# Bringing attention sums back to rows of nodes through DRAM and VectorE instead of TensorE transposes

## The chip, the cores and the metric

The kernel runs on one core of a Trainium2 chip. Its engines are TensorE (PE in the profile, with its weight loads as PEld), VectorE (DVE), ScalarE (ACT), GpSimd (POOL) and SyncE (SP, which here only issues transfers). The metric is the device time of one execution in microseconds (us), the median of several runs; lower is better.

## The reference, cut to what matters

Two layers act on x, which is 16 batches of 1024 nodes with 256 channels, all float32. The first is a graph convolution with two batch norms; the second is an attention with 4 heads of 64 channels. Each ends in a residual and a layer norm.

```python
def _L1_gnn_ref(x, para, adj, kv_w):
    ...                                    # g: the graph product, relu
    q = transpose(g).reshape(B, N, 4, 64).transpose(0, 2, 1, 3)
    kv = (x @ kv_w).reshape(B, N, 2, 4, 64).transpose(2, 0, 3, 1, 4)
    k, v = kv[0], kv[1]
    attn = softmax(einsum('bhnd,bhmd->bhnm', q, k) * scale)
    out = einsum('bhnm,bhmd->bhnd', attn, v)
    return out.transpose(0, 2, 1, 3).reshape(B, N, C)

x = _layernorm(x + _L0_gnn_ref(x, adj, ...))    # layer 0
x = _layernorm(x + _L1_gnn_ref(x, para, adj, kv_w))   # layer 1
```

The change touches the end of layer 1: what happens between the product of exponentials and values, and the last layer norm.

## The kernel before

A batch is worked on in two halves of 512 queries (`hf`), a half in two pairs of heads (`pair`), and a pair in four steps. In a step PE computes scores for two blocks of 128 keys, ACT takes exponentials (`e`), DVE adds them into `acc` (the denominators), and PE multiplies them with the values. The result `o` has channels on the partitions and queries along the row. The layer norm needs it the other way round, with nodes on the partitions, so `finish_a` turns it with four PE transposes for every 256 queries, and DVE multiplies the turned tile (in PSUM) with the reciprocal denominators.

```python
def scores(g): ...      # PE: s <- kT, qT, 64x64 blocks
def exps(g): ...        # ACT: e <- exp(s), 6 buffers of e
def sums(g):            # DVE: acc += e, two adds of 128x1024 per step
    ...
        nc.vector.tensor_add(ACC[b, hf, pair], ACC[b, hf, pair], E[g, a])

def attend(g):          # PE: o <- v, e
    ...
    if cp == NT // 2 - 1:                       # after a pair's four steps
        t = otp.tile([P, FB], F32, tag=f"ot{pair}", bufs=2 - pair, ...)
        o = O.pop((b, hf, pair))
        nc.scalar.copy(t, o[0])
        nc.vector.tensor_add(t, o[1], t)
        OT[b, hf, pair] = t

def dens(b, hf): ...    # PE: pd <- acc (sums over partitions); ACT: dt <- pd
def recips(b, hf): ...  # PE: pr <- dt (transposes); DVE: RD <- 1 / pr

def finish_a(b, j):     # j: 256 queries
    hf, k = divmod(2 * j, KB)
    p = ps_t.tile([P, 2, C], F32, tag="t", name="pf")
    for a in range(2):
        for pair in range(NP):
            nc.tensor.transpose(p[:, a, ts(pair, P)], OT[b, hf, pair][:, ts(k + a, P)], ident)
    r = ...
    nc.vector.tensor_mul(r, p, RD)              # 128x512, p in PSUM
    (nc.gpsimd if b < B - 1 else nc.vector).tensor_add(r, r, x1s.pop((b, j)))

def finish_s(b, j): ... # DVE: mean and variance of r; POOL: rs, nm
def finish_b(b, j): ... # ACT: r <- normalised; SP: out <- r
```

The normalised input of a later batch already takes another way into rows. Layer 0 leaves it in DRAM as `yT` with channels outside and nodes inside; `load` fetches it in pieces of 32 numbers so that each 32x32 block lies on the right partitions, POOL scales it (`bn2_q`), and one DVE instruction turns every 32x32 block (`rows`):

```python
y_blk = [yT_all[b].rearrange("i (d e) (q n) -> q e (i d) n", e=Q, q=NQ) for b in range(B)]  # Q = 32

def fetch_rows(b, j):   # called by load
    for q in range(NQ):
        nc.sync.dma_start(yts[b, j][q * Q : (q + 1) * Q]..., y_blk[b][q][:, ts(j, 2 * C // Q), :])
    nc.sync.dma_start(xrs[b, j], x[b, ts(j, 2 * P), :]...)

def bn2_q(b, j): ...    # POOL: yt <- yt * s, yt <- yt + t, 128x512 each
def rows(b, j):
    nc.vector.transpose(x1s[b, j], yts[b, j])
    nc.vector.tensor_add(x1s[b, j], x1s[b, j], xrs[b, j])
```

The pieces of later batches (`load`, `bn2_q`, `rows`, the gates `wg`, keys, values and the graph product) and the ends of earlier halves are put between groups of four steps by a hand-made schedule. A half batch ends every 8 steps. After the second half of a batch comes the stretch with the gates of the next batch and the loads and rows of the one after it; after the first half come only graph products, transposes of x1 and the ends. Every engine keeps its order of instructions, and all transfers are issued in order by SP.

Of the kernel before, what the change touches and what calls it, by code (L numbers as in the profile page):

```python
# [9 lines left out]
F32 = mybir.dt.float32  # L10
# [6 lines left out]
P = 128  # L17
# [5 lines left out]
def gnn_norm_attention_kernel(  # L23
# [16 lines left out]
    nc = tc.nc  # L40
    B, N, C = x.shape
    H = W1.shape[0]
    NT = N // P
    CT = C // P
    HT = H // P
    FB = 512
    NH = N // FB
# [4 lines left out]
    dram = ctx.enter_context(tc.tile_pool(name="dram", bufs=1, space=DRAM))  # L52
    ctx.enter_context(tc.manual_schedule())

    ident = const.tile([P, P], F32, name="ident")
# [25 lines left out]
    Q = 32  # L81
    NQ = P // Q
    y_blk = [yT_all[b].rearrange("i (d e) (q n) -> q e (i d) n", e=Q, q=NQ) for b in range(B)]
    st2_dram = dram.tile([2, C], F32, name="st2_d")

    c_dram = [dram.tile([NT, P], F32, name=f"crow_d{b}") for b in range(B)]
# [33 lines left out]
    with ExitStack() as l0:  # L120
# [32 lines left out]
        with ExitStack() as ph1:  # L153
# [9 lines left out]
            for i in range(0, NT, 2):  # L163
                t = hp.tile([P, 2, N], F32, tag="h", name=f"A{i}")
# [22 lines left out]
            KB = FB // P  # L187
# [6 lines left out]
            for h in range(NH):  # L194
                rows = range(h * KB, (h + 1) * KB)
                for i in rows:
                    blk = A[i][:, ts(i, P)]
# [8 lines left out]
                for j in range(NT):  # L206
                    p = ps.tile([P, FB], F32, tag="ah"[j % 2], name="pat")
# [25 lines left out]
            for c in range(HT):  # L233
                p = ps.tile([P, FB], F32, tag="a", name="pw1")
# [3 lines left out]
            for c in range(CT):  # L238
                p = ps.tile([P, FB], F32, tag="a", name="pw2")
# [120 lines left out]
            def hidden(b, h, f):  # L360
                p = ps.tile([P, FB], F32, tag="h", name="ph")
                for k in range(CT):
                    nc.tensor.matmul(
                        p,
                        W1T[:, k, ts(f, P)],
                        aggT[b][:, k, ts(h, FB)],
                        start=(k == 0),
                        stop=(k == CT - 1),
                    )
                return p  # L370
# [11 lines left out]
            for f in range(HT):  # L382
                for h in range(NH):
# [3 lines left out]
                    p = hidden(B - 1, h, f)  # L387
# [51 lines left out]
        with ExitStack() as ph2:  # L439
# [74 lines left out]
            for k, pair in enumerate(pairs):  # L514
# [4 lines left out]
                if not ahead:  # L519
                    for j in range(LDP):  # L520
                        load(0, j)
                    for j in range(LDP, NT // 2):
                        t = accp.tile([P, 2, FB], F32, tag="acc", name=f"first{j}")
# [14 lines left out]
    NP = HEADS // 2  # L538
# [17 lines left out]
    def fast():  # L556
      with ExitStack() as fx:
# [9 lines left out]
        otp = pool("otp", 3)  # L567
# [3 lines left out]
        ps_t = pool("ps_t", 4, space=PSUM)  # L571

        x1s, x1Ts, css, crows, mvs, wgs = {}, {}, {}, {}, {}, {}
        kTs, qTs, vs, S, E, ACC, O, OT, DT = {}, {}, {}, {}, {}, {}, {}, {}, {}
# [152 lines left out]
        def step(g):  # L727
            b, s = divmod(g, NS)
            hf, pair, cp = s // (NP * NT // 2), s // (NT // 2) % NP, s % (NT // 2)
            return b, hf, pair, cp  # L730
# [22 lines left out]
        def sums(g):  # L753
# [4 lines left out]
            else:  # L758
                for a in range(2):
                    nc.vector.tensor_add(ACC[b, hf, pair], ACC[b, hf, pair], E[g, a])  # L760

        def attend(g):
            b, hf, pair, cp = step(g)
            if cp == 0:
                O[b, hf, pair] = [ps_t.tile([P, FB], F32, tag="t", name=f"o{g}_{r}") for r in range(2)]
            for a in range(2):
                cb = 2 * cp + a
                for r in range(2):
                    for h in range(2):
                        nc.tensor.matmul(  # L770
                            O[b, hf, pair][r][h * HD : (h + 1) * HD, :],
                            vs[b][r * HD : (r + 1) * HD, cb, pair * P + h * HD : pair * P + (h + 1) * HD],
                            E[g, a][r * HD : (r + 1) * HD, h, :],
                            start=(cb == 0),
                            stop=(cb == NT - 1),
                        )
                E.pop((g, a))
            if cp == NT // 2 - 1:
                t = otp.tile([P, FB], F32, tag=f"ot{pair}", bufs=2 - pair, name=f"ot{g}")
                o = O.pop((b, hf, pair))  # L780
                nc.scalar.copy(t, o[0])  # L781
                nc.vector.tensor_add(t, o[1], t)  # L782
                OT[b, hf, pair] = t

        def dens(b, hf):
            p = ps_t.tile([P, FB], F32, tag="t", name="pd")
# [10 lines left out]
        KB = FB // P  # L797

        def recips(b, hf):
# [5 lines left out]
                RD[:, i : i + KB, :], p.rearrange("p k (h r) -> p k h r", r=32)[:, :, :, 0]  # L805
            )

        def finish_a(b, j):
            hf, k = divmod(2 * j, KB)
            p = ps_t.tile([P, 2, C], F32, tag="t", name="pf")  # L810
            for a in range(2):
                for pair in range(NP):
                    nc.tensor.transpose(p[:, a, ts(pair, P)], OT[b, hf, pair][:, ts(k + a, P)], ident)  # L813
            pool_r = (rp, "r") if b < B - 1 else (x1p, "x1")
            r = pool_r[0].tile([P, 2, C], F32, tag=pool_r[1], name=f"r_{b}_{j}")
            rd = RD[:, b * NT + 2 * j : b * NT + 2 * j + 2, :].rearrange("p a h -> p (a h)")
            nc.vector.tensor_mul(  # L817
                r.rearrange("p a (h d) -> p (a h) d", h=HEADS),
                p.rearrange("p a (h d) -> p (a h) d", h=HEADS),
                rd.unsqueeze(2).to_broadcast([P, 2 * HEADS, HD]),  # L820
            )
            (nc.gpsimd if b < B - 1 else nc.vector).tensor_add(r, r, x1s.pop((b, j)))  # L822
            R[b, j] = r
# [52 lines left out]
        def put(w, t, f, *a):  # L876
            at.setdefault(w * NC + t, []).append((f, a))
# [4 lines left out]
        for b in range(B):  # L882

            for hf in range(NH):
                t = (hf + 1) * (NC // NH)
                put(b, t, dens, b, hf)
                put(b, t + 1, recips, b, hf)
                for k in range(KB // 2):
                    put(b, t + 1 + k, finish_a, b, hf * (KB // 2) + k)
                    put(b, t + 1 + k, finish_s, b, hf * (KB // 2) + k)  # L890
                    late = NC - t - 2 - k if b == B - 1 and hf == 0 else 0
                    put(b, t + 2 + k + late, finish_b, b, hf * (KB // 2) + k)
            if b == 0:
                continue

            put(b - 2, 2, begin, b)
            for j in range(NT // 2):
                put(b - 2, j, load, b, j)
                put(b - 2, j + 1, bn2_q, b, j)
                put(b - 2, j + 2, rows, b, j)  # L900
                put(b - 2, j + 2, ln1_a, b, j)
                put(b - 2, j + 3, ln1_b, b, j)
                put(b - 2, j + 4, x1_t, b, j)
            put(b - 2, NC - 2, means, b)
            put(b - 2, NC - 1, crow, b)

            i = 0
            for t, n in enumerate(WG):
                for i in range(i, i + n):
                    put(b - 1, t, wg_a, b, i)  # L910
                    put(b - 1, t, wg_b, b, i)
                i += 1
            kv = [(keys, (b, c, h)) for c in range(CT) for h in range(NH)]
            kv += [(values, (b, j)) for j in range(0, NT, 2)]
            for t, n in enumerate(KV):
                for _ in range(n):
                    f, a = kv.pop(0)
                    put(b - 1, t, f, *a)
            m = 0
            for t, n in enumerate(QG):  # L920
                for m in range(m, m + n):
                    put(b - 1, NC - len(QG) + t, graph, b, m)
                m += 1
# [3 lines left out]
        nsteps = B * NS  # L927


        order = (dens, recips, finish_a, finish_b, x1_t, rows, ln1_a, ln1_b, finish_s, means, load, crow)  # L930
        rank = {f: k for k, f in enumerate(order)}
        short = (dens, recips, finish_a, x1_t, crow)
        long = (keys, values, graph)

# [120 lines left out]
        for t in range(min(at) // 2, max(max(at) // 2, nsteps // NK - 1) + 1):  # L1055
            g = NK * t
            now = [p for s in (2 * t, 2 * t + 1) for p in [(opening, (s,))] + arrange(at.get(s, []))]
            behind = max((k + 1 for k, fa in enumerate(now) if fa[0] in short), default=0)
            for k in range(len(now) + 1):
                if k == behind and 0 <= g < nsteps:  # L1060
                    sums(g)
                if k < len(now):
                    f, a = now[k]
                    f(*a)
            for k in range(g, g + NK):
                if 0 <= k + 1 < nsteps:
                    scores(k + 1)
                    exps(k + 1)
                if 0 <= k < nsteps:
                    if k > g:  # L1070
                        sums(k)
                    attend(k)
# [6 lines left out]
        )  # L1079

    flag = fast()


# [153 lines left out]
```

## Time and profile before

| | before |
|---|---|
| time, median of 3 runs | 2548.84 us (2546.09 to 2551.68) |
| span of the profiled execution | 2546.3 us |
| PE busy | 2487.9 us, 98% |
| DVE busy | 1730.6 us, 68% |
| ACT busy | 1078.3 us, 42% |
| POOL busy | 865.3 us, 34% |
| transfers | 233,349 packets, 163.79 MB, 21.1% of 16 engines' span on SP's queue |

Busy time is the union of an engine's instructions; share is of the span. The profile's groups list instructions of one source line together, with the tile written and the tiles read (`acc<-acc,e`), the mean duration of one and the idle time of the engine ahead of them with what ended it. The timeline lists the same instructions in order of time, with equal neighbours merged. Matmuls are pipelined, so what one costs PE is read from the distance of starts, not from its duration.

### The profile page before, as it was taken

How to read it: one execution, taken by the hardware profiler on the slowest of the kernel's cores; microseconds unless marked ns; L12 is line 12 of the kernel's file. 1: busy time of each engine (PE TensorE's matmuls, PEld its weight loads, DVE VectorE, ACT ScalarE, POOL GpSimd, SP SyncE). 2: the span in 40 equal slices, each digit the busy share in tenths (PEclk: the TensorE clock that was granted, in tenths of full speed). 3: DMA queues.
4: the chain of work that ended last, by engine and by line, in shares of the span. 5: the costliest groups of instructions: out<-in, count | busy, mean ns of one | idle time of the engine just before them, and what ended most of it. 6: DMA issues, size and time to landing. Idle time of an engine off the chain costs nothing. (4 is left out here: it accounts for less than half of the span.)

```text
span 2546.3 us, 33280 instructions
## 1 busy us (share of the span) xinstructions
PE 2487.9 (98%) x12813; PEld 1067.4 (42%) x12813; DVE 1730.6 (68%) x2594; ACT 1078.3 (42%) x1385; POOL 865.3 (34%) x766
## 2 busy tenths in 40 slices
PE   8999999998998999999999999999999999999997
PEld 4444444443443444344443444434444344443432
DVE  5545554556776776786877768777687776877556
ACT  2000000004453455465554655546556465564644
POOL 2222322222555323342433324333243332432132
PEclk9999999999999999999999999999999999999998
DMA  3122222230885201111111111111111111110000
GB/s 132 66 89 93 99 74 91 83 141 21 301 297 173 59 18 46 43 29 34 26 46 46 26 34 26 46 46 26 34 26 46 47 25 34 27 48 27 9 13 23
DMA packets 233349, 163.79 MB, mean 64 GB/s; under 512 B 136680, under 2 KB 221280, under 8 KB 226016
## 3 DMA queue, kind: packets, MB, share of 16 engines
q1 hardware_dynamic: 233184, 161.60, 21.1%
q8 instruction: 103, 1.69, 0.3%
q14 instruction: 62, 0.51, 0.1%
HBM read 98.58 MB, written 62.98 MB: 63 GB/s over the span
## 5 line engine op out<-in xcount | busy, mean ns | idle before, releaser
L751 ACT ACTIVATE e<-s 128x1024 f32<-128x1024 f32 x512 | 495.8, 1020 | 361.9 <-PE s L739 311.5
L760 DVE TENSOR_TENSOR acc<-acc,e 128x1024 f32<-128x1024 f32 x384 | 515.8, 1343 | 72.7 <-ACT e L751 42.6
L739 PE MATMUL s<-qT,kT 64*64 64x512 f32 x4096 | 492.4, 596 | 13.9 <-ACT e L751 13.2
L770 PE MATMUL o<-e,v 64*64 64x512 f32 x4096 | 486.4, 590 | 0.0
L713 PE MATMUL pg<-wg,x 128*128 128x512 f32 x960 | 434.5, 594 | 0.0
L822 POOL TENSOR_TENSOR r<-r,x 128x512 f32<-128x512 f32 x60 | 105.7, 1761 | 572.3 <-ACT wg L671 261.1
L739 PEld LDWEIGHTS s<-qT,kT 64*64 64x64 f32 x4096 | 147.2, 133 | 309.6 <-issue 250.9
L770 PEld LDWEIGHTS o<-e,v 64*64 64x64 f32 x4096 | 157.0, 133 | 284.1 <-issue 271.4
L599 POOL TENSOR_TENSOR yt<-yt,stq 128x512 f32<-128x512 f32 x120 | 192.4, 1603 | 193.2 <-DMA yt<-yT 188.3
L713 PEld LDWEIGHTS pg<-wg,x 128*128 128x128 f32 x960 | 172.3, 190 | 175.9 <-issue 166.1
L98 ACT COPY u<-pa 128x512 f32<-128x512 f32 x15 | 8.8, 585 | 475.3 <-PE pa L303 475.3
L680 DVE SCALAR_TENSOR_TENSOR wg<-wg,adj_sb 128x1024 f32<-128x1024 f32 x128 | 156.3, 1239 | 67.3 <-ACT wg L676 65.0
L303 PE MATMUL pa<-AhT,x 128*128 128x512 f32 x360 | 161.8, 592 | 0.0
L688 PE MATMUL pk<-x1T,kvw 128*128 128x512 f32 x256 | 118.4, 606 | 1.3 <-DVE x1T L639 1.3
L639 ACT COPY x1T<-px 128x512 f32<-128x512 f32 x60 | 35.1, 586 | 191.4 <-PE px L638 190.6
L699 PE MATMUL pv<-kvw,x1T 128*128 128x256 f32 x512 | 115.7, 379 | 0.0
L721 DVE TENSOR_TENSOR qT<-pg,para_sb 128x512 f32<-128x512 f32 x64 | 44.2, 690 | 101.7 <-PE pg L713 100.8
L334 PE MATMUL ph<-agg,SW 128*128 128x512 f32 x240 | 112.8, 592 | 0.0
L66 POOL TENSOR_SCALAR rs_a<-mv_a 128x2 f32<-128x2 f32 x64 | 20.5, 320 | 258.3 <-DVE mv_a L548 258.3
L303 PE MATMUL pa<-T,sx 128*128 128x512 f32 x240 | 107.9, 592 | 0.0
L303 PEld LDWEIGHTS pa<-AhT,x 128*128 128x128 f32 x360 | 68.4, 190 | 86.1 <-issue 86.1
L782 DVE TENSOR_TENSOR ot<-o,ot 128x512 f32<-128x512 f32 x64 | 44.0, 688 | 87.8 <-ACT ot L781 87.8
(193 smaller groups left out, 3332.4 us busy)
## 6 DMA issues: line engine op xcount, KB each, us to landing
h<-hT SPq DMA_DIRECT2D x28, 1024.0 KB, 4.4
hL<-h SPq DMA_DIRECT2D x28, 1024.0 KB, 9.2
x<-in_x_dram SPq DMA_DIRECT2D x16, 1024.0 KB, 7.3
yT<-y SPq DMA_DIRECT2D x64, 256.0 KB, 2.5
out_dram<-r SPq DMA_DIRECT2D x64, 256.0 KB, 2.1
xr<-in_x_dram SPq DMA_DIRECT2D x62, 256.0 KB, 2.9
yt<-yT SPq DMA_DIRECT2D x240, 64.0 KB, 2.9
crow<-crow_d SPq DMA_DIRECT2D x15, 512.0 KB, 4.0
```

Of the source, the lines that this page charges most:

```text
L303: nc.tensor.matmul(p, xs[n][:, k, :], bs[n][:, k, :], start=(k == 0), stop=(k == KN - 1))
L334: nc.tensor.matmul(p, ws[n][:, ts(f, P)], bs[n], start=True, stop=True)
L599: nc.gpsimd.tensor_tensor(y, y, sc, op)
L680: nc.vector.scalar_tensor_tensor(t, t, 1.0, adj_sb[:, i, :], op0=OP.add, op1=OP.mult)
L688: nc.tensor.matmul(p, kvw[:, k, ts(c, P)], x1Ts[b][:, k, ts(h, FB)], start=(k == 0), stop=(k == CT - 1))
L699: nc.tensor.matmul(p[:, ts(a, C)], x1Ts[b][:, k, ts(j + a, P)], kvw[:, k, C:], start=(k == 0), stop=(k == CT - 1),)
L713: nc.tensor.matmul(pg[b], x1s[b, k // 2][:, k % 2, ts(c, P)], wgs[b, k][:, ts(h, FB)], start=(k == 0), stop=(k == NT - 1))
L739: nc.tensor.matmul(t[r * HD : (r + 1) * HD, h, :], kTs[b, pair][h * HD : (h + 1) * HD, ts(2 * cb + r, HD)], qTs[b, pair, hf][h * HD : (h + ...
L751: nc.scalar.activation(E[g, a], S.pop((g, a)), AF.Exp)
L760: nc.vector.tensor_add(ACC[b, hf, pair], ACC[b, hf, pair], E[g, a])
L770: nc.tensor.matmul(O[b, hf, pair][r][h * HD : (h + 1) * HD, :], vs[b][r * HD : (r + 1) * HD, cb, pair * P + h * HD : pair * P + (h + 1) * HD],
L822: (nc.gpsimd if b < B - 1 else nc.vector).tensor_add(r, r, x1s.pop((b, j)))
```

## The change

Sums of values take the way that the input of a batch already takes. The finished tile `ot` goes from SBUF to a DRAM tile `o`, is read back in pieces of 32 numbers so that its 32x32 blocks lie on the right partitions, and one DVE instruction turns all blocks. This is meant to free PE from the four transposes of each `finish_a`. Only the second half of the last batch keeps the PE transposes, since nothing is left there to hide a way through DRAM. The second buffer of `ot0` is given up and its room taken by `ob`, the tile that is read back.

```diff
+    o_dram = {(b, h): dram.tile([NT // NH, C, P], F32, name=f"o{b}_{h}") for b in range(B) for h in range(NH)}
...
+        def by_pe(b, hf):
+            return b == B - 1 and hf == NH - 1
...
             if cp == NT // 2 - 1:
-                t = otp.tile([P, FB], F32, tag=f"ot{pair}", bufs=2 - pair, name=f"ot{g}")
+                t = otp.tile([P, FB], F32, tag=f"ot{pair}", bufs=1, name=f"ot{g}")
...
-                OT[b, hf, pair] = t
+                if by_pe(b, hf):
+                    OT[b, hf, pair] = t
+                else:
+                    nc.sync.dma_start(
+                        o_dram[b, hf][:, ts(pair, P), :].rearrange("i p n -> p i n"),
+                        t.rearrange("p (i n) -> p i n", n=P),
+                    )
...
+        def fetch_o(b, j):
+            hf, k = divmod(2 * j, KB)
+            if by_pe(b, hf):
+                return
+            t = OB[b, j] = otp.tile([P, 2, C], F32, tag="ob", bufs=1, name=f"ob{b}_{j}")
+            blk = o_dram[b, hf].rearrange("i (d e) (q n) -> q e (i d) n", e=Q, q=NQ)
+            for q in range(NQ):
+                nc.sync.dma_start(
+                    t[q * Q : (q + 1) * Q].rearrange("p a (d n) -> p (a d) n", n=Q),
+                    blk[q][:, ts(k // 2, 2 * C // Q), :],
+                )
...
         def finish_a(b, j):
...
+            if by_pe(b, hf):
+                p = ps_t.tile([P, 2, C], F32, tag="t", name="pf")
+                ...                                     # the four PE transposes
+            else:
+                p = r
+                nc.vector.transpose(r..., OB.pop((b, j))...)
             nc.vector.tensor_mul(r, p, RD)              # p is now r itself, in SBUF
...
                 for k in range(KB // 2):
+                    put(b, t + k, fetch_o, b, hf * (KB // 2) + k)
                     put(b, t + 1 + k, finish_a, b, hf * (KB // 2) + k)
...
-        order = (dens, recips, finish_a, finish_b, x1_t, rows, ln1_a, ln1_b, finish_s, means, load, crow)
+        order = (dens, recips, finish_a, fetch_o, finish_b, x1_t, rows, ln1_a, ln1_b, finish_s, means, load, crow)
```

More of the change, by code (lines that the diff above doesn't have):

```diff
@@ L806, in recips @@
             )
+        OB = {}
+        def fetch_o(b, j):
[9 more added lines that the diff above has]
+                )
         def finish_a(b, j):
             hf, k = divmod(2 * j, KB)
[L810 to L813, printed above, removed]
             pool_r = (rp, "r") if b < B - 1 else (x1p, "x1")
             r = pool_r[0].tile([P, 2, C], F32, tag=pool_r[1], name=f"r_{b}_{j}")
+            if by_pe(b, hf):
+                p = ps_t.tile([P, 2, C], F32, tag="t", name="pf")
+                for a in range(2):
+                    for pair in range(NP):
+                        nc.tensor.transpose(p[:, a, ts(pair, P)], OT[b, hf, pair][:, ts(k + a, P)], ident)
+            else:
+                p = r
+                nc.vector.transpose(
+                    r.rearrange("p a c -> p (a c)"), OB.pop((b, j)).rearrange("p a c -> p (a c)")
+                )
             rd = RD[:, b * NT + 2 * j : b * NT + 2 * j + 2, :].rearrange("p a h -> p (a h)")
```

## The prediction

> **What bounds the kernel now.** I read the page's shares first, then PE's waits, then the groups by shape, and last the timelines of PE and DVE over one batch in the middle (1618 to 1723 us; one batch takes 1723.34 - 1617.54 = 105.8 us from its second-half denominators to the next). The page:
>
> ```profile
> PE 2487.9 (98%) x12813; PEld 1067.4 (42%) x12813; DVE 1730.6 (68%) x2594; ACT 1078.3 (42%) x1385; POOL 865.3 (34%) x766
> ...
> PE   8999999998998999999999999999999999999997
> ...
> DVE  5545554556776776786877768777687776877556
> ```
>
> PE is busy in nearly every slice, DVE at about 0.7 in the attention slices. PE's longest listed wait is small:
>
> ```profile
> PE s L739 <- ACT e L751: 13.2, 16, 4.8
> ```
>
> That is 13.2 us in the whole run, so at first sight PE alone sets the time, and whatever is taken from PE is won. The groups by shape give the durations for the sums below (columns: busy us, mean ns of one, idle us ahead):
>
> ```profile
> L760 DVE TENSOR_TENSOR acc<-acc,e 128x1024 f32<-128x1024 f32 x384 | 515.8, 1343 | 72.7 <-ACT e L751 42.6
> ...
> L604 DVE TENSOR_TENSOR x<-x,xr 128x512 f32<-128x512 f32 x60 | 53.5, 891 | 2.1
> ...
> L817 DVE TENSOR_TENSOR r<-pf,RD 128x512 f32<-128x512 f32 x64 | 43.8, 684 | 39.3 <-PE pf L813 39.2
> ...
> L603 DVE STREAM_TRANSPOSE x<-yt 128x512 f32<-128x512 f32 x60 | 42.1, 702 | 0.0
> ...
> L813 PE MATMUL pf<-ident,ot 128*128 128x128 f32 x256 | 40.2, 280 | 0.0
> ```
>
> But the timeline of PE shows a second limit. It holds the stretch after a second half (from 1618):
>
> ```profile
> 1642.77 0.66 PE L813 MATMUL pf<-ident,ot 128*128 128x128 f32 x4
> 1643.26 5.35 PE L699 MATMUL pv<-kvw,x1T 128*128 128x256 f32 x24
> ...
> 1665.87 1.90 PE L770 MATMUL o<-e,v 64*64 64x512 f32 x16
> 1667.70 2.12 PE L791 MATMUL pd<-acc,ones 128*32 128x512 f32 x8
> 1669.75 0.66 PE L638 MATMUL px<-ident,x 128*128 128x128 f32 x4
> ```
>
> The denominators' matmul pd takes 2.12 us here and 1.07 us elsewhere (at 1617.54 and 1723.34). It is waiting for the last acc. DVE in the same stretch:
>
> ```profile
> 1627.18 1.22 DVE L680 SCALAR_TENSOR_TENSOR wg<-wg,adj_sb 128x1024 f32<-128x1024 f32 x1 [1.12 <-ACT wg L676]
> 1628.32 0.68 DVE L817 TENSOR_TENSOR r<-pf,RD 128x512 f32<-128x512 f32 x1
> ...
> 1631.31 0.43 DVE L547 BATCH_NORM_STATS2 st_z<-r 128x6 f32<-128x256 f32 x1 [1.17 <-POOL r L822]
> ...
> 1645.10 0.68 DVE L817 TENSOR_TENSOR r<-pf,RD 128x512 f32<-128x512 f32 x1
> ...
> 1659.53 9.18 DVE L760 TENSOR_TENSOR acc<-acc,e 128x1024 f32<-128x1024 f32 x6
> 1668.63 0.68 DVE L782 TENSOR_TENSOR ot<-o,ot 128x512 f32<-128x512 f32 x1
> ...
> 1676.03 0.26 DVE L804 RECIPROCAL RD<-pr 128x16 f32<-128x16 f32 x1 [2.32 <-PE pr L802]
> 1679.05 0.69 DVE L817 TENSOR_TENSOR r<-pf,RD 128x512 f32<-128x512 f32 x1 [2.76 <-PE pf L813]
> ```
>
> From 1631.31 to 1673 DVE has no gap at all, and its acc ends at 1668.71, after PE has arrived at 1667.70. So between 1631 and 1669 **DVE is the bound**, by a hair, and PE by a hair less. After the first half (1669 to 1723) DVE waits 2.32 and 2.76 us for PE: there PE is the bound. The 2.12 us form of pd stands in the timeline once per batch, 13 times in all, in the batches whose stretch holds the loads and rows of a batch two ahead.
>
> [...] L604, with both inputs in SBUF, goes from 691 up to 1269 ns, mean 891, while L817, whose pf is in PSUM, stays at 679 to 692. [...] Pieces of 32 numbers are 128 B; the trace has the same pattern already (the two groups below), at a small price.
>
> **The change, part by part.**
>
> Taken from PE: 64 - 2 = 62 groups of four transposes. By distance of starts one group costs 1626.38 - 1625.94 = 0.44 us (first of a half) or 1643.26 - 1642.77 = 0.49 us (second). 31 x 0.44 + 31 x 0.49 = 28.8 us.
>
> Added to DVE: 62 block transposes. L603 is the same instruction, 0.70 us: 43 us of busy time. The multiplication now reads r from SBUF instead of pf from PSUM: alone 0.69 as before, beside POOL like L604, so up to +0.2 us. DVE busy 1731 to about 1780.
>
> Added transfers: per half two stores of 256 KB and eight fetches of 64 KB. The existing pairs are:
>
> ```profile
> yT<-y SPq DMA_DIRECT2D x64, 256.0 KB, 2.5
> ...
> yt<-yT SPq DMA_DIRECT2D x240, 64.0 KB, 2.9
> ```
>
> SP needs about 0.5 us to issue each fetch (four in 2.1 us). So after ot (end 1618.95): store landed about 1621.3, four fetches issued by 1623.4 and landed by about 1626, since in the trace POOL starts on a fetched tile 4.05 us after the first of its four issues (1655.61, 1659.66). DVE wants the tile at 1628.3. After a first half it is 1669.3 + 7.1 = 1676.4 against a slot of 1676.3 to 1679. **The way through DRAM is hidden**, with up to about 2 us to spare.
>
> Moved: SP issues in order, and the loads of the batch two ahead stand behind the store and the first fetch. Before they were issued at 1603; now from 1623.4, landing about 1627.4. POOL's two bn2_q (1.6 to 2.0 us each) then run until about 1631.2 ahead of POOL's add of r (2.1 us), which before ended at 1631.28 and now at about 1633.4. DVE's schedule also changes: one gate (0.66 + 1.2 us) now stands ahead of the st_z that waits for it, and fills that wait. DVE: transpose 1628.3, multiplication (contended) to 1630.0, acc 1631.2, gate 1633.1, st_z 1633.4 to 1634.5, second gate, accs from 1635.7. Before: 1635.37. So the first block transpose of this stretch costs only about 0.3 us, because it falls where DVE waited anyway.
>
> The second transpose (at 1645) has no such gap: +0.74 us. POOL's later work overlaps more of the six accs, which are slowed by it (9.2 us contended, 7.9 us for six in the other half): +0.3 to 0.4. DVE's chain in this stretch thus grows by D = 0.3 + 0.75 + 0.35 = about 1.4 us, and PE, who had two groups of transposes less there (0.93 us), waits for it.
>
> Sum: of the 62 groups 26 (2 x 13) lie in those stretches and give nothing; the other 36 give 28.8 - 13 x 0.93 = 16.7 us. Against that stand 13 x 1.4 = 18.2 us of longer DVE chain. Net **+1.5 us: 2550 us**.
>
> **Rivals.**
>
> *PE is the bound everywhere.* Then all 28.8 us are won: 2520 us. For it: 98% busy, waits of 13 us. Against it: the long pd and the gapless DVE stretch. If D were 0, 2532 us.
>
> *The transfer is late, and DVE, in order, stands before it with everything behind.* Each microsecond costs 13 in the stretches after second halves; after first halves DVE has gaps. Fetches and loads now queue together (eight fetches in 4 us), and a row copy in front (crow) slowed such a set to 5.2 us in the trace. Two us late: 2576 us.
>
> *POOL becomes the gate.* If the loads land at 1629 instead of 1627.4, r, st_z and the accs come 1.6 us later, and 13 x 1.6 = 21 us are lost: 2571 us. I take this as the likeliest way to be wrong upwards.
>
> **Range and chances.** D decides. At D = 0 it is 2532, at 1.4 it is 2550, at 3.5 it is 2578. With some room below for waits on PE that go away too: 2528 to 2580. Two per cent is 51 us; faster than 2498 needs more than PE can give (28.8 us), so 0.03; slower than 2600 needs D above 5, so 0.05; within 0.92.
>
> **What would show it.** PE's busy time down by about 29 us and its idle time up by about as much; waits of PE for DVE (acc at pd, or wg at the graph product pg) appearing once per batch in the stretch after a second half; that stretch (1617.5 to 1669.8, 52.2 us) longer by about 1.4 us and the rest of the batch (53.6 us) shorter by about 0.9; DVE's transposes of ob at about 702 ns with little wait for the DMA; DVE's multiplication near 0.75 to 0.9 us. If DVE waits for ob, or PE's idle time stays as it was, the steps above are wrong.

## The result and the profile after

The change makes the kernel slower: **2580.48 us** (median of 4 runs, 2578.87 to 2581.23) against 2547.47 us beside it (2546.06 to 2551.68). The ratio is 1.0126 [1.0108, 1.0144]. That is within 2%, as predicted, but 30 us above the predicted 2550, at the upper edge of the range (2580). The profiled spans are 2546.3 and 2577.0 us.

The page after the change, busy time by engine and VectorE's row of tenths:

```profile
PE 2469.6 (96%) x12565; PEld 1045.0 (41%) x12565; DVE 1790.3 (69%) x2656; ACT 1078.1 (42%) x1385; POOL 872.0 (34%) x766
...
DVE  5555555457676778686876868768687686876656
```

PE has 248 matmuls less (62 groups of four transposes) and is 18 us less busy, but the span is 31 us longer, so its idle time has grown by 49 us. The waits of PE say for whom (us in all, times, longest):

```profile
PE pg L714 <- DVE wg L681: 35.6, 13, 3.3
PE s L740 <- ACT e L752: 24.1, 16, 9.4
...
PE pd L803 <- DVE acc L761: 3.4, 3, 3.0
```

The first entry is new: the graph product waits for VectorE's gates 13 times, once in each batch that loads another one. The waits for ScalarE's exponentials were there before, 13.2 us in all and 4.8 at most; now one of them is 9.4 us long. Where do these waits stand? The distances of the denominators' matmul pd cut each trace into stretches (starts; "stretch" is from a second half's pd to the first half's, "rest" from there to the next second half's):

| | before | after, 5 of 13 batches | after, 8 of 13 |
|---|---|---|---|
| stretch with the loads | 50.16 | 52.59 | 54.26 |
| rest of the batch | 55.64 | 54.81 | 53.76 |
| batch | 105.80 | 107.40 | 108.02 |

The three columns are the usual batch of each kind (two pauses of about 3.3 and 2.9 us in the first group of five add some tenths). Over the 13 batches the sum is 1375.8 us before and 1402.4 after, +26.6. Outside them, up to the first of these batches the kernel gains 1.3 + 0.8 = 2.1 us, and after the last it loses 194.14 - 187.96 = 6.2 us. These add up to the 30.7 us of the spans. The 1.3 us stand ahead of the first pd (926.71 against 927.99 us), where two kernels that are alike up to there can differ as much (928.25 us with the added matmuls below), so they need not come from the change.

The next fence is PE's timeline in one batch of the last column (start, duration, operation; in brackets the wait ahead and what ended it):

```profile
1519.95 1.06 PE L803 MATMUL pd<-acc,ones 128*32 128x512 f32 x8
...
1557.59 1.13 PE L714 MATMUL pg<-wg,x 128*128 128x512 f32 x2 [2.67 <-DVE wg L681]
1558.65 3.32 PE L740 MATMUL s<-qT,kT 64*64 64x512 f32 x16
...
1574.24 1.06 PE L803 MATMUL pd<-acc,ones 128*32 128x512 f32 x8
```

After the pause a group of 16 score matmuls takes 3.32 us; elsewhere it takes 1.90 to 1.95. Its clock, by windows (stretch and length; busy us of PE, PEld, DVE, ACT, POOL; granted clock; DMA share; GB/s):

```profile
1555.00:1557.50 2.50, 0.00 (x0) 0.00 (x0) 2.43 (x6) 0.00 (x0) 2.37 (x3) 1.00 0.53 132
1557.50:1560.00 2.50, 2.41 (x10) 0.77 (x14) 2.46 (x4) 1.16 (x3) 2.40 (x4) 0.82 0.03 7
1560.00:1562.50 2.50, 2.50 (x16) 0.80 (x12) 2.40 (x10) 2.36 (x3) 1.95 (x4) 0.50 0.51 135
```

PE was idle in the first window and was then granted half its clock, by these windows for about (1 - 0.82) x 2.5 / 0.5 + 2.5 = 3.4 us. This is what tells the two columns apart: in 8 of the 13 batches the pause is followed by half speed, in 5 it is not, even where the pause was the longest (3.30 us). Note that the time at half speed counts as busy, so that PE's busy time fell by only 18 us.

VectorE in the same stretch (same columns as PE's timeline):

```profile
1530.73 0.70 DVE L845 STREAM_TRANSPOSE r<-ob 128x512 f32<-128x512 f32 x1
1531.47 0.80 DVE L849 TENSOR_TENSOR r<-r,RD 128x512 f32<-128x512 f32 x1
1532.19 2.07 DVE L758 TENSOR_TENSOR acc<-e,e 128x1024 f32<-128x1024 f32 x1
1534.18 1.76 DVE L674 TENSOR_SCALAR wg<-wg 128x1024 int32<-128x1024 int32 x1
...
1539.31 9.35 DVE L761 TENSOR_TENSOR acc<-acc,e 128x1024 f32<-128x1024 f32 x6
1549.18 0.70 DVE L845 STREAM_TRANSPOSE r<-ob 128x512 f32<-128x512 f32 x1
...
1564.37 9.18 DVE L761 TENSOR_TENSOR acc<-acc,e 128x1024 f32<-128x1024 f32 x6
```

The block transposes start at their slot, 0.70 us each and without a wait for the DMA; in none of the 13 stretches does one wait. The way through DRAM is hidden here. But the chain that begins at pd ends 1564.37 + 9.18 - 1519.95 = 53.60 us later. Before it ended 1659.53 + 9.18 - 1617.54 = 51.17 us later. **VectorE's chain has grown by 2.43 us, not by the predicted 1.4.** The first acc took 2.07 us and the gate's first instruction 1.76 us. Before, in the stretch from 1617.54, they took 1.22 and 0.66 us, and the six accs behind them began 17.83 us after pd in place of 19.36:

```profile
1628.92 1.22 DVE L757 TENSOR_TENSOR acc<-e,e 128x1024 f32<-128x1024 f32 x1
...
1632.40 0.66 DVE L673 TENSOR_SCALAR wg<-wg 128x1024 int32<-128x1024 int32 x1
...
1635.37 9.21 DVE L760 TENSOR_TENSOR acc<-acc,e 128x1024 f32<-128x1024 f32 x6
```

What GpSimd did in the changed kernel meanwhile:

```profile
1529.69 3.49 POOL L600 TENSOR_TENSOR yt<-yt,stq 128x512 f32<-128x512 f32 x2 [28.37 <-DMA yt<-yT]
1533.14 2.25 POOL L854 TENSOR_TENSOR r<-r,x 128x512 f32<-128x512 f32 x1
```

It scaled the loaded rows until 1533.18, beside most of the long acc, and then added x to r until 1535.39, beside most of the slow gate. In the batches without half speed pd usually starts 52.59 us after the last pd, 1.01 us before VectorE's chain ends (53.60), and has its long form (2.12 us): its second half needs the last acc. In the others PE comes about 0.6 us after the chain (54.26), and pd has its short form.

The two transfers, in the list of DMA issues (KB each, median us from issue to landing):

```profile
o<-ot SPq DMA_DIRECT2D x62, 256.0 KB, 2.3
...
ob<-o SPq DMA_DIRECT2D x248, 64.0 KB, 2.1
```

In the 13 batches the longest wait of a block transpose for its transfer is 2.00 us; it stands after a first half, and the rest of that batch is no longer for it (53.75 us). Only at the end of the run do the transfers show. VectorE's two longest waits for one, and two waits of PE:

```profile
2491.98 0.71 DVE L845 STREAM_TRANSPOSE r<-ob 128x512 f32<-128x512 f32 x1 [4.81 <-DMA ob<-o]
...
2533.79 0.71 DVE L845 STREAM_TRANSPOSE r<-ob 128x512 f32<-128x512 f32 x1 [4.36 <-DMA ob<-o]
```
```profile
2513.64 3.69 PE L740 MATMUL s<-qT,kT 64*64 64x512 f32 x16 [9.43 <-ACT e L752]
...
2558.67 1.46 PE L803 MATMUL pd<-acc,ones 128*32 128x512 f32 x4 [3.00 <-DVE acc L761]
```

The first of these waits of PE: at 2511.58 ScalarE's normalisation of r had waited 8.88 us for GpSimd's nm, which needs that r, and the exponentials stood behind it (2512.58). From pd to pd this stretch takes 41.90 us instead of 38.95. The second: VectorE's last accs end late behind its wait of 4.36 us for ob, the last pd takes 5.51 us instead of 1.08, and from its start to the end of the run it is 22.43 us instead of 16.45. The other pieces of the end are 2.7 us shorter together.

### The profile page after: what moved, and what is told of

Same layout as the page of the kernel before. It is cut to its first block, busy times and chain, and to the rows that moved or that the text cites. A ratio compares the mean times of both kernels' runs of the same rounds, so it can differ in the third digit from the quotient of the medians.

```text
span 2577.0 us, 33374 instructions
## 1 busy us (share of the span) xinstructions
PE 2469.6 (96%) x12565; PEld 1045.0 (41%) x12565; DVE 1790.3 (69%) x2656; ACT 1078.1 (42%) x1385; POOL 872.0 (34%) x766
## 4 chain that ended last, share of the span: by engine, by line
PE 54%; DVE 15%; ACT 2%; issue 2%; DMA 1%; POOL 0%; SPq 0%; DVEq 0%; ACTq 0%; POOLq 0%
PE pg L714 14%; PE s L740 13%; PE o L776 12%; PE po L480 7%; DVE acc L761 5%; PE pk L689 3%; DVE wg L681 2%; DVE acc L758 1%; PE pd L803 1%; DVE wg L674 1%; PE px L639 1%; PE pg L1039 1%; DVE st_z L548 1%; ACT wg L676 1%; DVE r L845 1%
## 5 line engine op out<-in xcount | busy, mean ns | idle before, releaser
L761 DVE TENSOR_TENSOR acc<-acc,e 128x1024 f32<-128x1024 f32 x384 | 509.3, 1326 | 78.6 <-ACT e L752 48.9
L740 PE MATMUL s<-qT,kT 64*64 64x512 f32 x4096 | 502.0, 606 | 24.8 <-ACT e L752 24.1
L714 PE MATMUL pg<-wg,x 128*128 128x512 f32 x960 | 438.3, 599 | 35.6 <-DVE wg L681 35.6
L600 POOL TENSOR_TENSOR yt<-yt,stq 128x512 f32<-128x512 f32 x120 | 175.7, 1464 | 415.2 <-DMA yt<-yT 409.6
L681 DVE SCALAR_TENSOR_TENSOR wg<-wg,adj_sb 128x1024 f32<-128x1024 f32 x128 | 162.4, 1279 | 64.6 <-ACT wg L677 62.3
L870 ACT ACTIVATE r<-r,nm,rs_z 128x256 f32<-128x256 f32 x128 | 69.9, 594 | 145.3 <-POOL nm L862 145.3
L700 PEld LDWEIGHTS pv<-kvw,x1T 128*128 128x128 f32 x512 | 96.0, 190 | 31.5 <-issue 19.4
```

The costliest lines, as they stand in the source:

```text
L600: nc.gpsimd.tensor_tensor(y, y, sc, op)
L681: nc.vector.scalar_tensor_tensor(t, t, 1.0, adj_sb[:, i, :], op0=OP.add, op1=OP.mult)
L700: nc.tensor.matmul(p[:, ts(a, C)], x1Ts[b][:, k, ts(j + a, P)], kvw[:, k, C:], start=(k == 0), stop=(k == CT - 1),)
L714: nc.tensor.matmul(pg[b], x1s[b, k // 2][:, k % 2, ts(c, P)], wgs[b, k][:, ts(h, FB)], start=(k == 0), stop=(k == NT - 1))
L740: nc.tensor.matmul(t[r * HD : (r + 1) * HD, h, :], kTs[b, pair][h * HD : (h + 1) * HD, ts(2 * cb + r, HD)], qTs[b, pair, hf][h * HD : (h + ...
```

## The experiments

**Theory A**, formed from these traces: the cost lies wholly in the ends of second halves, in VectorE's chain of that stretch, plus the end of the run. **Rival B**: the way through DRAM is late in every half. **Rival C**: the block transposes cost wherever they stand, because VectorE is too full. **Rival D**: the half-speed clock after the pause is the loss, not the chain. Two kernels ask where, five ask what, and one puts the answers together. All times are medians; ratios are to the kernel before, run beside them (2546.91 us for the first four, 2549.09 us for the others). Where medians of two changed kernels are subtracted, this shift of 2.2 us is not taken out, so such differences hold to about 2 us; the distances in the traces are finer.

**Only the first halves take the new way.** (In this and the next one, and where the last three half batches keep the PE transposes, the buffers of `ot` are shared out anew so that everything fits.)

```diff
-            return b == B - 1 and hf == NH - 1
+            return b == B - 1 or hf == NH - 1
```

> Only the first half of each batch (but the last) goes through DRAM; second halves keep the PE transposes. Theory A (the loss lies in the stretch after a second half, where VectorE and GpSimd set the time): the first halves win on PE 15 x 0.93 us = 14 us and nothing is lost elsewhere: about 2533 us, and PE's wait for the gate wg at the graph product is gone. Theory B (the way through DRAM is late and VectorE waits for it everywhere): no gain or a loss here too, 2547 us or more. Theory C (VectorE's 0.7 us transposes cost the time wherever they stand): 2547 us or more.

Measured: 2534.71 us, 0.9952 [0.9936, 0.9969]. The batch takes 50.14 + 54.81 = 104.95 us: the stretch as before, the rest 0.83 less. B and C fall, since both would have cost here too; that the transfer is late in second halves alone is answered by the trace, where no block transpose of those 13 stretches waits for it. The transposes taken from PE are won where PE is the bound.

**Only the second halves take it.**

```diff
-            return b == B - 1 and hf == NH - 1
+            return b == B - 1 or hf == 0
```

> Only the second half of each batch (but the last) goes through DRAM; first halves keep the PE transposes. Theory A: the whole loss is here, about 3.1 us in each of 13 batches plus some 3 us at the end, less 2 us: about 2590 us. Theories B and C: half of the loss of the full change, about 2563 us.

Measured: 2590.7 us, 1.0174 [1.0157, 1.0191]. The two parts add up: -12.2 and +43.8 make +31.6, and the whole change is +33.0. PE's waits for the gates are all here (36.1 us, 13 times, against none listed with the first halves alone), and half speed follows in 10 of the 13 batches.

**The first two of the four loads of the batch two ahead go ahead of the store and the fetches** in SyncE's order, so that GpSimd scales those rows earlier.

```diff
-                put(b - 2, j, load, b, j)
+                put(b - 2, j if j > 1 else -1, load, b, j)
```

> The full change, but the first two loads of the batch two ahead are issued one unit earlier, ahead of the store and fetches of ot. Theory A in its form 'the loads queue behind the store and fetch, so GpSimd's scaling and its add of r run late and hold VectorE's acc and gate': those two VectorE instructions fall from 2.07 and 1.76 us back to about 1.2 and 0.7, PE's wait for wg falls from 2.7 us to about 1 us per batch, 2580 falls to between 2535 and 2560 us (2535 if the half-speed stretch after the wait goes too). Theory C (the added VectorE work alone makes wg late): 2575 us or more.

Measured: 2562.78 us, 1.0066 [1.0049, 1.0083]. VectorE and GpSimd in the stretch, two timelines of this kernel:

```profile
1524.77 1.22 DVE L758 TENSOR_TENSOR acc<-e,e 128x1024 f32<-128x1024 f32 x1
1525.90 1.76 DVE L674 TENSOR_SCALAR wg<-wg 128x1024 int32<-128x1024 int32 x1
```
```profile
1524.98 2.13 POOL L854 TENSOR_TENSOR r<-r,x 128x512 f32<-128x512 f32 x1 [23.39 <-issue]
```

The acc is back at 1.22 us, and the chain ends 52.64 us after pd instead of 53.60: 0.96 us less. The gate stays at 1.76, which was not expected: the add of r moved forward with it. The pause of PE falls from 2.67 to 1.70 us, and half speed follows in one batch of 13 instead of 8. Batches of 106.44 us instead of 107.40 give 13 x 0.96 = 12.5 us, and seven batches less at half speed give 7 x 0.62 = 4.3; together 16.8 of the 17.7 us between the medians. So the loads' place in SyncE's queue was about half of the whole loss of 33.0 us.

**Three extra matmuls fill PE's pause** (their result is not used), which leaves VectorE's work alone.

```diff
+            if m == 5 and 2 <= b <= 14:
+                fill = ps_t.tile([P, FB], F32, tag="t", name="fill")
+                for _ in range(3):
+                    nc.tensor.matmul(fill, x1s[b, 0][:, 0, ts(c, P)], wgs[b, 0][:, ts(h, FB)], start=True, stop=True)
             nc.tensor.matmul(
```

> The full change, with three extra 128x512 matmuls (2.6 us) into a scratch PSUM tile just ahead of the graph product that waits for the gate wg; their result is not used. If PE's half speed after the pause comes from the pause, PE stays at full speed and 13 x 1.9 = 25 us are won though PE does more work: about 2556 us. If the half speed has another cause (VectorE, GpSimd or ACT holding the matmuls), it stays at about 2580 us.

Measured: 2575.04 us, 1.0112 [1.0095, 1.0129], an interval that overlaps that of the change. This was a miss: a gain of some 20 us was expected and about 5 came. PE's timeline:

```profile
1557.67 1.95 PE L744 MATMUL s<-qT,kT 64*64 64x512 f32 x16
...
1571.57 2.11 PE L807 MATMUL pd<-acc,ones 128*32 128x512 f32 x8
```

Half speed is gone from every batch, but pd is back in the long form, where it waits for acc. Each batch takes 107.40 us, exactly what the changed kernel's batches without half speed take. So rival D falls as the main cause, and its cost is measured: 108.02 - 107.40 = 0.62 us in each of 8 batches, 5.0 us in all. The other 1.6 us per batch are VectorE's.

**The last three half batches keep the PE transposes**, instead of only the last one.

```diff
-            return b == B - 1 and hf == NH - 1
+            return b * NH + hf >= B * NH - 3
```

> The full change, but the last three half batches (not only the last one) keep the PE transposes. Theory: of the 31 to 33 us that the change lost, about 6 lie at the end, where the way through DRAM has no gates, loads or rows beside it and VectorE and ACT wait for it (PE's wait of 9.4 us for e, and 3 us at pd). They go, and four groups of transposes (1.9 us) come back: about 2576 us. Rival: the end costs nothing by itself: 2582 us.

Measured: 2572.19 us, 1.0094 [1.0077, 1.0111]. The part of the span after the last of the 13 batches falls from 194.1 to 185.6 us, and PE's longest wait for e from 9.4 to 4.8 us, as in the kernel before:

```profile
PE s L740 <- ACT e L752: 19.4, 16, 4.8
```

So 8.5 us are won at the end, against 8.3 between the medians: the loss of 6.2 us there comes from the way through DRAM in those half batches. Both places go back: the stretch with ScalarE's late row takes 37.89 us instead of 41.90, and the time from the last pd on 16.75 instead of 22.43. This run does not part the two.

**The second group of 256 queries of a second half is finished two places of the schedule later**, behind the next first half, where VectorE has gaps.

```diff
+                    hold = 2 if (hf, k) == (NH - 1, 1) and not by_pe(b, hf) else 0
-                    put(b, t + 1 + k, finish_a, ...)      # finish_s and finish_b likewise
+                    put(b, t + 1 + k + hold, finish_a, ...)
```

> The full change, but the second group (j = 3) of a second half is finished two units later, in the stretch after the next first half, where VectorE has gaps; this takes 2.4 us (block transpose 0.74, multiplication 0.6, statistics 1.1) from VectorE's gapless stretch and changes no work. Theory A (VectorE's chain in that stretch sets the time): the chain is as long as before the change again, PE's wait for wg falls below 1 us, and 13 x about 3 us are won: about 2540 us. Rival D (GpSimd's late scaling and the DMA queue set it, VectorE's length does not matter): 2575 us or more.

Measured: 2525.83 us, 0.9910 [0.9893, 0.9926], better than expected. This expectation's Rival D is not the D above: it has GpSimd's late scaling and the DMA queue set the time whatever the length of VectorE's chain, and it falls, with 2575 us or more expected. PE's waits for exponentials are 3.1 us at most, and its waits for the gates, 35.6 us in the changed kernel, are down to 1.2:

```profile
PE s L740 <- ACT e L752: 17.5, 16, 3.1
```

The usual batch takes 49.87 + 54.58 = 104.45 us, 2.95 less than 107.40 though only one transpose (0.70) and the multiplication and the reductions with it were moved by two places. VectorE's chain ends 50.60 us after pd instead of 53.60. The first 1.5 us that it had grown by are still there (the six accs begin at 19.34 us, 19.36 in the changed kernel); the later part of the chain is what became shorter. VectorE executes the same instructions; they stand in another stretch. GpSimd's add of r moved along with them, and two adds of rows beside GpSimd became shorter (from 1.03 and 1.26 to 0.69 and 0.80 us), so some 0.8 of the 3.00 us lies in them. The expectation left the end at its +6 us; it fell from 194.1 to 183.7 us as well. The row that ScalarE had waited for there, at 2511.58, is the second group of batch 14's second half, and so is moved too; that this is the reason is read from the trace, and no run tests it alone.

**Loads first, second group late and three half batches by PE, together.**

> Loads first, the second group of a second half finished late, and the last three half batches by PE. By theory A VectorE's chain is then about 1 us shorter than before the change, so PE is the bound nearly everywhere, and the wait at pd is mostly gone as well: 2515 to 2525 us.

Measured: **2516.59 us, 0.9875 [0.9859, 0.9892]**, faster than both kernels. The page, and pd in PE's timeline:

```profile
PE 2449.9 (97%) x12581; PEld 1044.6 (42%) x12581; DVE 1783.7 (71%) x2652; ACT 1077.3 (43%) x1385; POOL 854.0 (34%) x766
```
```profile
1757.34 1.07 PE L811 MATMUL pd<-acc,ones 128*32 128x512 f32 x8
```

pd has the short form and the batch takes 49.65 + 53.81 = 103.46 us. VectorE's chain ends 49.62 us after pd, 0.03 us before PE gets there, so PE is the bound in both stretches, by a hair in this one, though VectorE is about as busy as in the changed kernel (1783.7 against 1790.3 us).

**One of GpSimd's adds of r goes to VectorE**, on top of the earlier loads.

```diff
-            (nc.gpsimd if b < B - 1 else nc.vector).tensor_add(r, r, ...)
+            (nc.gpsimd if b < B - 1 and j != 2 else nc.vector).tensor_add(r, r, ...)
```

> Loads first, and GpSimd's add of x1 to r for the first group of a second half is done by VectorE instead. If VectorE's gate instruction of 1.76 us is long because that GpSimd add holds it off, it falls to 0.7 us, VectorE pays 0.7 us for the add and saves 1.1: about 0.4 us per batch, 2558 us against 2563. If the 1.76 us have another cause, the gate stays and 2571 us is to be expected.

Measured: 2558.28 us, 1.0035 [1.0021, 1.0049]. The gate's first instruction, by shape (busy, mean ns, idle ahead):

```profile
L674 DVE TENSOR_SCALAR wg<-wg 128x1024 int32<-128x1024 int32 x64 | 43.7, 683 | 22.1 <-ACT wg L672 22.1
```

In the changed kernel its mean was 919 ns. VectorE has been given an add and is done earlier: the batch takes 106.08 us instead of 106.44 (0.36 x 13 = 4.7; 4.5 us between the medians). It is GpSimd's instruction beside it that had slowed the gate. A slow gate need not cost anything: with the first halves alone its mean is 927 ns, and there it falls where VectorE had waited for r before, so that the stretch stays at 50.14 us.

## Why the prediction was right and where it was wrong

**Right.** That the time stays within 2%, and the structure: PE is the bound in the rest of a batch and VectorE in the stretch with the loads. The groups after first halves paid nearly as sized (0.83 us a batch, sized at 0.44 + 0.49 = 0.93), those in the stretch gave nothing, and the way through DRAM was hidden in the middle. The order of events came as predicted: the block transpose at pd + 10.78 us (predicted 10.76), GpSimd's scaling at pd + 9.74 (9.86), the end of its add at pd + 15.44 (15.86). The second transpose cost 0.76 us (0.75 in the sum).

**Wrong: the step "the first block transpose of this stretch costs only about 0.3 us".** It cost 19.36 - 17.83 = 1.53 us, counted from pd to the start of the accs. At this point the prediction let the multiplication alone pay for GpSimd's shifted work, and gave acc 1.2 us and the gate's two instructions 1.9 us. The multiplication was hardly slowed (mean 717 ns), but acc took 0.85 us more and the gate's first instruction 1.1 us more; the wait for st_z absorbed a part. The earlier loads took 0.96 us of it away, and the add on VectorE another 0.36. What was missed is that these two also ran beside GpSimd's shifted work: acc ends 1.08 us after GpSimd's scaling, the gate 0.55 us after GpSimd's add, so each ran past its neighbour by less than its usual length (1.22 and 0.66 us). That both were held until GpSimd was done would fit these ends, but no run shows it. The prediction had such a slowing in front of it (L604, from 691 up to 1269 ns) and, here, applied it to one instruction out of three. The later overlap, put at 0.35, was only 0.14. The prediction's D, the growth of VectorE's chain, was thus 1.53 + 0.76 + 0.14 = 2.43, and 13 x (2.43 - 1.4) = 13.4 us of the miss come from it.

**Missed: what a pause does to PE's clock.** 8 x 0.62 = 5.0 us. The half speed itself costs about 1.7 us (pause to pd: 16.65 us against 14.95 when PE is at full speed), of which pd's short form gives 1.05 back.

**Wrong: the ten groups outside the 13 batches.** They were counted as pure gain, 16.7 - 13 x 0.93 = 4.6 us. At the start 2.1 us came, at the end 6.2 us were lost: a net loss of 4.1, so 8.7 us of the miss. The would-show list spoke of VectorE waiting for ob; it does six times, but the two long waits (4.81 and 4.36 us) stand in the last two batches.

The three make 27.1 of the 29.2 us between the predicted +1.5 and the measured +30.7 of the spans. Another 13 x 0.10 = 1.3 us are the groups after first halves, which paid 0.83 instead of 0.93 us; the rest lies in the few pauses that were longer than usual. The upper edge of the range, 2580 us, had been worked out with D = 3.5 alone. D was 2.43; the clock and the end, which the prediction did not have as costs, brought the time there. That the edge fits is luck.

**The rivals.** PE as the only bound is refuted by the run with the second halves alone, which lost 43.8 us; the late transfer by the block transposes, none of which waits for its transfer in the 13 stretches. "POOL becomes the gate" named the right engine for the wrong reason: the rows landed when expected and GpSimd finished earlier than thought; what it did was to slow VectorE's instructions beside it (acc from 1.22 to 2.07 us, the gate from 0.66 to 1.76). PE's busy time fell by 18 us and not 29, mainly because it contains 8 x 1.7 us of half speed.

## What to carry to other kernels

Find which engine's chain ends each stretch before moving work onto that engine, and move it to a stretch where the engine has gaps: the same 62 block transposes cost 33 us in one order and gave 23 us in another (32 us with the loads first and two half batches fewer on the new way). When a transfer is put into a queue, ask what is issued behind it, when that work will now run, and which instructions of other engines it will run beside. The ends of a run have no other work to hide in and want their own sum.

## What the runs showed of the hardware that was not expected

A pause of PE can be followed by half its clock, and of pauses of one length some are and some are not. In the changed kernel half speed followed 8 of the 11 pauses of about 2.67 us and neither of the two longer ones (2.92 and 3.30 us). With the second halves alone it followed 8 of 11 such pauses and both of 3.3 us. With the loads first it followed 1 of 13 pauses of 1.70 us, and with the add on VectorE none of 13 of 1.35 us. In the windows above half speed lasted about 3.4 us behind a pause of 2.67 us. What decides besides the pause's length is left open.

A VectorE instruction can take much longer beside a GpSimd instruction: the int32 gate of 128x1024 took 1.76 instead of 0.66 to 0.70 us beside an add of 2.13 to 2.25 us, acc 2.07 instead of 1.22 beside the scaling of rows (two instructions, 3.49 us).

The long form of pd costs PE about 1.05 us in the rest of the batch (54.81 against 53.76). The starts of its eight matmuls show where: in the short form four start within 0.02 us and the other four 0.45 us later; in the long form they start in twos, at 0, 0.45, 1.07 and 1.52 us, the last four behind the late acc. In some batches the second four start about 1.3 us after the first, where acc is later still.
